# A planned decoder-layer kernel: intermediate values written over their inputs, and buffer rings of new sizes

## The chip, the cores and the metric

The kernel runs on one core of a Trainium2 chip. The time is the device time of one launch in microseconds. Three runs of the kernel before gave 1340.83, 1343.05 and 1343.17 us, a median of 1343.05. A profile was taken of one more execution, whose time was 1342.45 us.

The names of engines in the profile: PE is the matrix engine (PEld its weight loads), DVE the vector engine, ACT the engine for activations, POOL the general engine (GpSimd), SP the engine that issues the DMAs.

## The reference

32 sequences of 128 tokens with 128 features, in fp32, go through one decoder layer with a layernorm behind each residual:

```python
x = _layernorm(x + _L0_attn_ref(x, L0_attn_weight))             # 16 heads, q = k = v = x, projected 2048 -> 128
x = _layernorm(x + _L0_xattn_ref(x, ctx_1024, ...))             # 16 heads, window of 64, biases, projection
x = _layernorm(x + _L0_ffn_ref(x, wqkv, ..., w1, b1, w2, b2))   # a stack of two layers, see below
```

Each of the two layers in the third line is: shift half of the features by one token, qkv, l2norm of q and k with a scale and rotary factors, local attention with 8 heads of 64, `x = x + o @ wo`; then again shift, layernorm, `a, g = split(h @ w1 + b1)`, `x = x + (a * gelu(g)) @ w2 + b2`.

## The kernel before, in words

The 32 sequences are cut into nine groups, `SIZES` (L21): seven of 4, one of 3, one of 1. A group goes through four stages, which are Python generators: `self_attention` (L528), `cross_attention` (L612), and `layer` (L953) for l = 0 and l = 1. Within a stage the work is done per sequence ("batch" in the code): `self_half` twice (L545), `cross_batch` (L678), `local_batch` (L766). What is done for a whole group at once is the loads, the transposes of the group, the layernorms (`layernorm`, L372), the projections and the feed-forward (`feed_forward`, L899). `finish` (L972) adds the residual around the two layers, normalises and stores.

Nothing is issued in the order in which it is written. Every step is entered into a plan by `op` (L80) with an engine, an estimated duration, and the values that it reads and writes. L992 to L1000 sort the stages' pieces into a list of priorities: a piece of stage k and group g stands at `STARTS[g]/G + k*LAG*CLOSE[g]`, and the pieces of one stage are drawn apart by `SPREAD[k]`. Then `Plan.issue` (L128) simulates the engines with the estimated durations, and at each step issues the operation that can start first; on one engine it takes the oldest of those that can start within `near` ns (default 80) of the first, and it looks no further than `ahead` operations past the oldest that is not yet issued (`AHEAD`, 250). The result is a fixed order for each engine.

A value (`Val`, L56) lives in a slot of a ring (`Ring`, L45), from the first operation that writes or holds it to the last that uses it. There are three rings that matter: `m`, the 8 PSUM banks, of which two are kept back; `big`, 18 SBUF buffers of 1032 floats, 5 kept back; `mid`, 19 SBUF buffers of 520 floats, 6 kept back. Two smaller ones hold whole groups: `xb` (x1 and the outcome of layer 0) and `xc` (x2), 4 each. "Kept back" is this test (L171):

```python
if len(q.free) < len(vs) + (0 if q.queue[q.head] in vs else q.keep):
    ok = False
```

An operation that needs new slots may take the last ones only for the value that is next in the ring's line; any other must leave `keep` slots free. So values out of line get at most 6 of `m`, 13 of `big` and 13 of `mid`.

The places that the change touches: the sum of the heads into `acc` (L605 to L609); the bias `yc` added to x1 into a new value `x1c` (L648), and the projection's sum into another `acc` (L669); the outcome of the attention of a layer, `xa` (L961, written in L893 to L897); in the feed-forward `xb = x + b2` (L901), then the shifted copy `h` (L907; the copy of the unshifted half is L739 on POOL, the shifted half is a matmul, L743, evicted in L747), `hn`, the layernorm of `h` (L908), and the sum into `dst` (L948); in `finish` a sum `acc` and an outcome `o` (L973).

Lines that come up in the prediction: L416 is the row maximum of the scores on DVE, L462 the exponentials of cross and local attention, L477 the transposes of the exponentials, L484 their eviction, L492 the masked copy of the eight heads (`eight_heads`), L507 the scores of self and cross attention, L554 and L583 the value product and the output product of self attention, L772 the qkv product, L789 the power of the norms on POOL, L800 the rotary product on POOL, L847 and L876 the scores and outputs of local attention, L922 and L942 the two products of the feed-forward.

Of the kernel before, what the change touches and what calls it, by code (L numbers as in the profile page):

```python
# [12 lines left out]
ALU = mybir.AluOpType  # L13
# [12 lines left out]

AHEAD = 250
LAG = 1.3  # L30
CLOSE = (1, 1, 1, 1, 1, 1, 1, 0.9, 0.95)
SPREAD = (1.3, 0.9, 0.7, 1.1)
LH, LD = 8, 64
INNER = LH * LD
HID = 341
# [192 lines left out]
def decoder_kernel(ctx: ExitStack, tc: tile.TileContext, a: dict, out: bass.AP):  # L228
# [6 lines left out]
    def ring(name, n, keep, shape, dtype=F32, pool=const):  # L235
        return Ring([pool.tile(shape, dtype, name=f"{name}{i}") for i in range(n)], keep)

    mring = ring("m", 8, 2, [P, 512], pool=ps)
    big = ring("big", 18, 5, [P, 1032])
    mid = ring("mid", 19, 6, [P, 520])  # L240
    vbring = ring("vb", 2, 1, [P, 4, 288])
    x1ring = ring("xb", 4, 1, [P, G, D])
    x2ring = ring("xc", 4, 1, [P, G, D])
    small = ring("sm", 24, 4, [P, 32])
    padring = ring("pad", 4, 1, [P, 2, 64], BF16)

# [125 lines left out]
    def layernorm(src, dst, n):  # L372
        st = Val(small)

        def stats():
            for j in range(n):
                nc.vector.bn_stats(st.t[:, 6 * j : 6 * j + 6], group(src.t)[:, j, :])

        op("DVE", n * 290, stats, [src], [st])
        mv = Val(small)  # L380

        def aggr():
            for j in range(n):
# [12 lines left out]

        op("POOL", 1100 + 260 * n, rest, [], [mv])

        def apply():
            x, y = group(src.t), group(dst.t)  # L400
            for j in range(n):
                nc.scalar.activation(
                    y[:, j, :], x[:, j, :], AF.Identity,
                    scale=mv.t[:, 8 + j : 9 + j], bias=mv.t[:, 12 + j : 13 + j],
                )

        op("ACT", 425 * n, apply, [src, mv], [dst])

    def two_banks():
        return [Val(mring, lambda t: t.rearrange("p (h k) -> p h k", h=4)) for _ in range(2)]  # L410
# [117 lines left out]
    def self_attention(g):  # L528
        xT = load_group(a["xt"], g)
        if g == 0:  # L530
            load_self()
        x0 = load_group(a["xg"], g)
        if g == 1:
            load_cross()
        acc, n = Val(mid), SIZES[g]
        for j in range(n):
            yT = eight_heads(xT, j)
            for hh in range(2):
                self_half(j, hh, x0, xT, acc, yT)
            yield  # L540
        x1 = Val(x1ring, lambda t: t.rearrange("p g d -> p (g d)"))
        layernorm(acc, x1, n)
        x1s[g] = x1

    def self_half(j, hh, x0, xT, acc, yT):  # L545

        zs = Val(big, lambda t: t.rearrange("p (h d) -> p h d", h=HH))
        op("POOL", 130, lambda: nc.gpsimd.memset(zs.t[:, :, D : D + 1], 1.0), [], [(zs, 2)])
# [52 lines left out]
        for n, ns in ((4, 1270), (2, 730), (1, 450)):  # L601
            op("POOL", ns,
               lambda n=n: nc.gpsimd.tensor_tensor(z(0, n), z(0, n), z(n, n), ALU.add),  # L603
               [], [zs], port=n > 1)
        y = lambda: group(acc.t)[:, j, :]  # L605
        first = lambda: group(x0.t)[:, j, :] if hh == 0 else y()
        op("POOL", 450,
           lambda: nc.gpsimd.tensor_tensor(y(), first(), z(0, 1)[:, 0, :], ALU.add),
           [zs, x0], [(acc, j)])  # L609


    def cross_attention(g):  # L612
# [30 lines left out]

        vT = Val(mid)
        op("PE", n * 228, values, [cT, w_cross], [vp], hold=[vT])
        op("ACT", 140 + 113 * n,
           lambda: nc.scalar.copy(vT.t[:, every], vp.t[:, every]), [vp], [vT])
        x1c = Val(mid)  # L648
        op("POOL", 316 * n,
           lambda: nc.gpsimd.tensor_tensor(  # L650
               group(x1c.t)[:, 0:n], group(x1.t)[:, 0:n],
               yc.unsqueeze(1).to_broadcast([P, n, D]), ALU.add),
           [x1, w_cross], [x1c], port=True)
        on = Val(mid)
        for j in range(n):
            cross_batch(j, qT, kT, vT, on)
            yield
        onT = turned(on, n)
        yp = Val(mring)

        def project():
            for j in range(n):
                nc.tensor.matmul(
                    yp.t[:, 128 * j : 128 * j + 128], group(onT.t)[:, j, :], woT,
                    start=True, stop=True,
                )

        op("PE", n * 228, project, [onT, w_cross], [yp])
        acc = Val(mid)  # L669
        op("DVE", 160 + 135 * n,  # L670
           lambda: nc.vector.tensor_tensor(
               acc.t[:, every], yp.t[:, every], x1c.t[:, every], ALU.add),
           [yp, x1c], [acc])
        x2 = Val(x2ring, lambda t: t.rearrange("p g d -> p (g d)"))
        layernorm(acc, x2, n)
        x2s[g] = x2

    def cross_batch(j, qT, kT, vT, on):  # L678
# [87 lines left out]
    def local_batch(l, j, xin, hT, xout):  # L766
# [119 lines left out]
        def project():  # L886
            for i in range(4):
# [2 lines left out]
                    start=(i == 0), stop=(i == 3),  # L890
                )

        op("PE", 4 * 228, project, [onT, w_layer[l]], [yp], hold=[xout])  # L893
        op("DVE", 290,
           lambda: nc.vector.tensor_tensor(
               group(xout.t)[:, j, :], yp.t[:, 0:D], group(xin.t)[:, j, :], ALU.add),
           [yp, xin], [(xout, j)])  # L897

    def feed_forward(l, xg, dst, n):  # L899
        every = slice(0, 128 * n)  # L900
        xb = Val(mid)  # L901
        op("POOL", 316 * n,
           lambda: nc.gpsimd.tensor_tensor(
               group(xb.t)[:, 0:n], group(xg.t)[:, 0:n],
               b2[l].unsqueeze(1).to_broadcast([P, n, D]), ALU.add),
           [xg, w_layer[l]], [xb], port=True)
        h = shifted(xg, n)  # L907
        hn = Val(mid)  # L908
        layernorm(h, hn, n)
        tp, hT = Val(mring), Val(mid)  # L910
        op("PE", 113 * n, turn(hn, tp, n), [hn], [tp], hold=[hT])
        op("DVE", 160 + 135 * n,
           lambda: nc.vector.tensor_scalar(
               hT.t[:, every], tp.t[:, every], cols[:, 2 + 2 * l : 3 + 2 * l],
# [24 lines left out]
        def project():  # L939
# [4 lines left out]
                        w2[l][:m, c, :], start=(c == 0), stop=(c == 2),  # L944
                    )

        op("PE", 3 * 228 * n, project, us + [w_layer[l]], [yp], hold=[dst])
        op("DVE", 160 + 135 * n,  # L948
           lambda: nc.vector.tensor_tensor(dst.t[:, every], yp.t[:, every], xb.t[:, every], ALU.add),
           [yp, xb], [dst])  # L950


    def layer(l, g, xin):  # L953
        if g == 0:
            if l + 1 < DEPTH:
                load_layer(l + 1)
            prepare_layer(l)
        n = SIZES[g]
        hT = turned_shifted(xin, n)
        last = l == DEPTH - 1  # L960
        xa = Val(mid)  # L961
        xf = Val(mid) if last else Val(x1ring, lambda t: t.rearrange("p g d -> p (g d)"))
        for j in range(n):
            local_batch(l, j, xin, hT, xa)
            yield
        feed_forward(l, xa, xf, n)
        if last:
            finish(g, xf, n)
        else:
            xfs[g] = xf  # L970

    def finish(g, xf, n):  # L972
        acc, o, every = Val(mid), Val(mid), slice(0, 128 * n)  # L973
        op("POOL", 316 * n,
           lambda: nc.gpsimd.tensor_tensor(
               acc.t[:, every], xf.t[:, every], x2s[g].t[:, every], ALU.add),
           [xf, x2s[g]], [acc], port=True)
        layernorm(acc, o, n)
        op("SP", P * 512 * n / 380,
           lambda: nc.sync.dma_start(  # L980
               out_dram[:, STARTS[g] : STARTS[g] + n], group(o.t)[:, 0:n]), [o], [])

# [14 lines left out]
    for _, k, g, stage in sorted(todo, key=lambda t: t[:3]):  # L997
        if (k, g) not in running:
            running[k, g] = stage(g)
        next(running[k, g], None)  # L1000
    plan.issue(ahead=AHEAD)


def _constants():
# [96 lines left out]
```

## Time and profile before

| what | value |
|---|---|
| median of three runs | 1343.05 us |
| the profiled execution: its time | 1342.45 us |
| its span, from the first to the last instruction | 1340.7 us |
| mean granted clock of PE | 0.987 |
| instructions | 25686 |

The page of the profile gives the busy time of each engine as a share of the span: PE 94%, DVE 76%, ACT 74%, POOL 67%, PEld 63%. The DMA engines are busy in the first slice (0.6) and next to nothing afterwards. The answers of the trace that are quoted further on are of four kinds: busy time per stretch of the span ("windows"), groups of equal instructions with the number, the busy time and the mean duration, the waits of an engine, and the chain that ended last, in pieces: start, duration, what, and how many instructions. The PE's matmul records overlap where they are pipelined, and their ends are modelled; the pace of a stretch without gaps is its length divided by its number of matmuls.

### The profile page before, as it was taken

The page shows a single profiled execution, that of the slowest core. Times are in us where ns is not written, and L with a number is a line of the kernel's source. Part 1 is how long each engine was busy: PE and PEld are TensorE (multiplying, and loading weights), DVE is VectorE, ACT ScalarE, POOL GpSimd, SP SyncE. Part 2 cuts the span into 40 slices and gives each one's busy share as a digit, 9 for nine tenths or more (in the row PEclk, how much of TensorE's full clock was granted, in tenths as well). Part 3 has the DMA queues.
Part 4 walks back from the last instruction along what each step waited for, and adds up shares of the span by engine and source line. Part 5 has one row for each costly group of instructions (what it writes and reads, how often), then busy time and mean ns, then how long its engine had stood idle before and what let it go on. Part 6 is the DMA issues. An engine that isn't in the chain of part 4 may idle for free.

```text
span 1340.7 us, 25686 instructions
## 1 busy us (share of the span) xinstructions
PE 1265.2 (94%) x9314; PEld 847.3 (63%) x9314; DVE 1020.6 (76%) x1963; ACT 992.4 (74%) x2841; POOL 900.5 (67%) x1070
## 2 busy tenths in 40 slices
PE   8899999999999998999999999999999989999986
PEld 4656666766666665756666665666665576676655
DVE  2656788688877877877876887778877887888673
ACT  4355676777778777787787877867878698998874
POOL 3794875777686757867786667685766554868543
PEclk9999999999999999999999999999999999999988
DMA  6000000000000000000000000000000000000000
GB/s 229 1 1 1 17 9 1 2 17 4 7 1 9 9 1 16 1 1 17 1 17 1 13 1 19 1 3 1 7 9 1 3 1 9 1 2 1 9 1 17
DMA packets 9118, 15.59 MB, mean 12 GB/s; under 512 B 672, under 2 KB 5536, under 8 KB 8736
## 3 DMA queue, kind: packets, MB, share of 16 engines
q1 hardware_dynamic: 8992, 13.95, 3.2%
q8 instruction: 74, 1.21, 0.4%
q14 instruction: 52, 0.43, 0.1%
HBM read 11.85 MB, written 2.10 MB: 10 GB/s over the span
## 4 chain that ended last, share of the span: by engine, by line
PE 65%; ACT 12%; DVE 11%; POOL 9%; issue 2%; DMA 0%; POOLq 0%; DVEq 0%; SPq 0%; ACTq 0%
PE m L772 8%; PE m L583 7%; PE m L507 7%; PE m L554 6%; PE m L477 6%; ACT big L462 5%; PE m L847 4%; PE m L876 4%; PE m L922 4%; PE m L700 3%; PE m L942 3%; PE m L888 3%; PE m L827 3%; DVE big L862 2%; DVE sm L416 2%; POOL sm L789 2%
## 5 line engine op out<-in xcount | busy, mean ns | idle before, releaser
L462 ACT ACTIVATE big<-m,sm 128x128 f32<-128x128 f32 x1024 | 320.8, 405 | 52.6 <-DVE sm L416 47.4
L416 DVE TENSOR_REDUCE sm<-m 128x4 f32<-128x512 f32 x384 | 244.9, 682 | 110.8 <-PE m L507 40.2
L800 POOL TENSOR_TENSOR big<-big,layer_w 128x512 f32<-128x512 f32 x128 | 166.3, 1300 | 86.8 <-ACT big L777 74.6
L603 POOL TENSOR_TENSOR big<-big 128x512 f32<-128x512 f32 (+2 forms) x192 | 163.5, 852 | 83.2 <-DVE big L593 31.5
L789 POOL TENSOR_TENSOR sm<-sm,nhalf 128x16 f32<-128x16 f32 x64 | 198.4, 3100 | 25.2 <-DVE sm L786 21.0
L772 PE MATMUL m<-layer_w,mid 128*128 128x512 f32 x384 | 188.6, 602 | 4.5 <-ACT big L462 2.3
L477 PE MATMUL m<-ident,big 128*128 128x128 f32 x1024 | 147.3, 280 | 26.5 <-DVE big L862 13.3
L477 PEld LDWEIGHTS m<-ident,big 128*128 128x128 f32 x1024 | 116.9, 143 | 76.5 <-issue 33.6
L492 POOL TENSOR_TENSOR big<-mid,self_w 128x1024 f32<-128x1024 f32 x64 | 126.5, 1982 | 15.1 <-ACT mid L629 9.1
L507 PE MATMUL m<-big,mid 64*128 64x512 f32 x512 | 134.5, 614 | 0.0
L583 PEld LDWEIGHTS m<-big,big 128*128 128x128 f32 x1024 | 121.6, 193 | 17.1 <-issue 5.2
L583 PE MATMUL m<-big,big 128*128 128x129 f32 x1024 | 129.6, 280 | 2.3 <-DVE big L593 2.3
L554 PE MATMUL m<-self_w,mid 128*128 128x512 f32 x256 | 124.7, 604 | 6.5 <-DMA self_w<-in_self_w 5.9
L462 ACT ACTIVATION_READ_ACCUMULATOR big<-m,sm 128x1 f32 x512 | 120.2, 235 | 0.0
L862 DVE TENSOR_TENSOR big<-big,sm 128x512 f32<-128x512 f32 x128 | 108.8, 850 | 4.4
L593 DVE TENSOR_TENSOR big<-m,sm 128x384 f32<-128x384 f32 (+1 forms) x192 | 98.6, 514 | 6.8 <-DVE sm L592 0.3
L561 ACT COPY big<-m 128x512 f32<-128x512 f32 x128 | 74.8, 596 | 36.3 <-PE m L554 35.0
L484 DVE COPY big<-m 128x512 f32<-128x512 f32 x128 | 82.2, 682 | 23.6 <-PE m L477 23.2
L484 ACT COPY big<-m 128x512 f32<-128x512 f32 x128 | 76.0, 605 | 31.3 <-PE m L477 29.8
L809 DVE TENSOR_TENSOR big<-big,layer_w 128x1024 f32<-128x1024 f32 x64 | 83.3, 1302 | 20.3 <-ACT big L777 18.6
L833 ACT COPY big<-m 128x512 f32<-128x512 f32 x128 | 71.4, 604 | 31.2 <-PE m L827 30.9
L772 PEld LDWEIGHTS m<-layer_w,mid 128*128 128x128 f32 x384 | 64.1, 190 | 47.1 <-issue 32.5
(112 smaller groups left out, 2488.9 us busy)
## 6 DMA issues: line engine op xcount, KB each, us to landing
layer_w<-in_layer_w SPq DMA_DIRECT2D x2, 1877.0 KB, 11.8
mid<-in_xt SPq DMA_DIRECT2D x7, 256.0 KB, 3.1
mid<-in_xg SPq DMA_DIRECT2D x7, 256.0 KB, 3.0
mid<-in_ct SPq DMA_DIRECT2D x7, 256.0 KB, 3.2
out<-mid SPq DMA_DIRECT2D x7, 256.0 KB, 2.3
self_w<-in_self_w SPq DMA_DIRECT2D x1, 516.0 KB, 4.5
self_w<-in_self_w SPq DMA_DIRECT2D x1, 512.0 KB, 5.9
cross_w<-in_cross_w SPq DMA_DIRECT2D x1, 329.5 KB, 6.8
```

Source lines behind the costliest of these rows:

```text
L416: lambda b=b: nc.vector.tensor_reduce(nm.t[:, 4 * b : 4 * b + 4], s[b].t, AX.X, ALU.max, negate=True),
L462: nc.scalar.activation(e.t[:, h, :], s[b].t[:, h - 4 * b, :], AF.Exp, bias=nm.t[:, h : h + 1], accum_out=sums.t[:, h : h + 1] if sums else ...
L477: nc.tensor.transpose(tp.t[:, 128 * c : 128 * c + 128], e.t[:, 4 * b + c, :], ident)
L484: lambda: copy(et.t[:, 4 * b : 4 * b + 4, :], tp.t.rearrange("p (c k) -> p c k", c=4)),
L507: nc.tensor.matmul(s[b].t, group(stationary.t)[r, j, :], moving.t[r, 4 * hh : 4 * hh + 4, :], start=True, stop=True, tile_position=(64 * b ...
L554: lambda zp=zp, h0=h0: nc.tensor.matmul(zp.t, group(xT.t)[:, j, :], attn_w[:, h0 : h0 + 4, :], start=True, stop=True),
L583: nc.tensor.matmul(oz.t[:, i, :], e.t[:, h0 + i, :], zs.t[:, h0 + i, :], start=True, stop=True,)
L603: lambda n=n: nc.gpsimd.tensor_tensor(z(0, n), z(0, n), z(n, n), ALU.add),
L772: lambda hp=hp, i=i: nc.tensor.matmul(hp.t, group(hT.t)[:, j, :], wqkv[l][:, INNER * i : INNER * (i + 1)], start=True, stop=True),
L789: nc.gpsimd.tensor_tensor(rn.t[:, 0:16], rn.t[:, 0:16], nhalf, ALU.pow)
L800: nc.gpsimd.tensor_tensor(r2.t[:, :, :, d0 : d0 + 32], q[:, :, :, d1 : d1 + 32], tabs[l][:, :, d0 : d0 + 32].unsqueeze(2).to_broadcast([P, ...
L862: nc.vector.tensor_tensor(e.t[:, 4 * b : 4 * b + 4, :], e.t[:, 4 * b : 4 * b + 4, :], r.unsqueeze(2).to_broadcast([P, 4, P]), ALU.mult)
```

## The change

- Values are written over an input. Self attention sums into `x0`, the loaded group, in place of `acc`; cross attention adds `yc` to `x1` and the projection to the same `x1`, which stays until the layernorm into x2 has read it; layer 1 (the second) writes its attention outcome over its input; layer 0 keeps `xa` as a new value, but in the ring `xb` rather than `mid`. In the feed-forward the layernorm of `h` is written over `h`, `b2` is added to x in place, and the sum goes to the same value. In `finish` the sum, the layernorm and the store use the one value.
- In the feed-forward the order of two steps is exchanged: the shifted copy `h` is entered before the sum with `b2`, which now writes over what the copy reads.
- The rings: `big` 18 to 22, `mid` 19 to 16 with 5 kept back rather than 6, `xb` 4 to 8, `xc` 4 to 6. In bytes of a partition: 18*4128 + 19*2080 + 8*2048 = 130208 before, 22*4128 + 16*2080 + 14*2048 = 152768 after. `m` stays at 8 with 2 kept back.
- The planner's settings: `AHEAD` 250 to 230, `near` 80 to 60, the last of `CLOSE` 0.95 to 0.9 (the group of one), the last of `SPREAD` 1.1 to 1.5 (layer 1).

No instruction is added or taken away, and none gets another shape.

```diff
-AHEAD = 250
+AHEAD = 230
 LAG = 1.3
-CLOSE = (1, 1, 1, 1, 1, 1, 1, 0.9, 0.95)
-SPREAD = (1.3, 0.9, 0.7, 1.1)
+RINGS = (22, 16, 8, 6)
+KEEP = (2, 5, 5)
+NEAR = 60
+CLOSE = (1, 1, 1, 1, 1, 1, 1, 0.9, 0.9)
+SPREAD = (1.3, 0.9, 0.7, 1.5)
...
-    mring = ring("m", 8, 2, [P, 512], pool=ps)
-    big = ring("big", 18, 5, [P, 1032])
-    mid = ring("mid", 19, 6, [P, 520])
+    mring = ring("m", 8, KEEP[0], [P, 512], pool=ps)
+    big = ring("big", RINGS[0], KEEP[1], [P, 1032])
+    mid = ring("mid", RINGS[1], KEEP[2], [P, 520])
...
-    x1ring = ring("xb", 4, 1, [P, G, D])
-    x2ring = ring("xc", 4, 1, [P, G, D])
+    x1ring = ring("xb", RINGS[2], 1, [P, G, D])
+    x2ring = ring("xc", RINGS[3], 1, [P, G, D])
...
-        op("ACT", 425 * n, apply, [src, mv], [dst])
+        op("ACT", 425 * n, apply, [mv] + ([src] if src is not dst else []), [dst])
...
-        y = lambda: group(acc.t)[:, j, :]
-        first = lambda: group(x0.t)[:, j, :] if hh == 0 else y()
+        y = lambda: group(x0.t)[:, j, :]
         op("POOL", 450,
-           lambda: nc.gpsimd.tensor_tensor(y(), first(), z(0, 1)[:, 0, :], ALU.add),
-           [zs, x0], [(acc, j)])
+           lambda: nc.gpsimd.tensor_tensor(y(), y(), z(0, 1)[:, 0, :], ALU.add),
+           [zs], [(x0, j)])
...
-        x1c = Val(mid)
         op("POOL", 316 * n,
            lambda: nc.gpsimd.tensor_tensor(
-               group(x1c.t)[:, 0:n], group(x1.t)[:, 0:n],
+               group(x1.t)[:, 0:n], group(x1.t)[:, 0:n],
                yc.unsqueeze(1).to_broadcast([P, n, D]), ALU.add),
-           [x1, w_cross], [x1c], port=True)
+           [w_cross], [x1], port=True)
...
-        xb = Val(mid)
+        h = shifted(xg, n)
         op("POOL", 316 * n,
            lambda: nc.gpsimd.tensor_tensor(
-               group(xb.t)[:, 0:n], group(xg.t)[:, 0:n],
+               group(xg.t)[:, 0:n], group(xg.t)[:, 0:n],
                b2[l].unsqueeze(1).to_broadcast([P, n, D]), ALU.add),
-           [xg, w_layer[l]], [xb], port=True)
-        h = shifted(xg, n)
-        hn = Val(mid)
-        layernorm(h, hn, n)
+           [w_layer[l]], [xg], port=True)
+        layernorm(h, h, n)
...
-        xa = Val(mid)
-        xf = Val(mid) if last else Val(x1ring, lambda t: t.rearrange("p g d -> p (g d)"))
+        xa = xin if last else Val(x1ring, lambda t: t.rearrange("p g d -> p (g d)"))
...
-    plan.issue(ahead=AHEAD)
+    plan.issue(ahead=AHEAD, near=NEAR)
```

More of the change, by code (lines that the diff above doesn't have):

```diff
@@ L534, in self_attention @@
             load_cross()
-        acc, n = Val(mid), SIZES[g]
+        n = SIZES[g]
         for j in range(n):
@@ L538, in self_attention, with self_half @@
             for hh in range(2):
-                self_half(j, hh, x0, xT, acc, yT)
+                self_half(j, hh, x0, xT, yT)
             yield
         x1 = Val(x1ring, lambda t: t.rearrange("p g d -> p (g d)"))
-        layernorm(acc, x1, n)
+        layernorm(x0, x1, n)
         x1s[g] = x1
-    def self_half(j, hh, x0, xT, acc, yT):
+    def self_half(j, hh, x0, xT, yT):
         zs = Val(big, lambda t: t.rearrange("p (h d) -> p h d", h=HH))
@@ L668, in cross_attention @@
         op("PE", n * 228, project, [onT, w_cross], [yp])
-        acc = Val(mid)
         op("DVE", 160 + 135 * n,
            lambda: nc.vector.tensor_tensor(
-               acc.t[:, every], yp.t[:, every], x1c.t[:, every], ALU.add),
-           [yp, x1c], [acc])
+               x1.t[:, every], yp.t[:, every], x1.t[:, every], ALU.add),
+           [yp], [x1])
         x2 = Val(x2ring, lambda t: t.rearrange("p g d -> p (g d)"))
-        layernorm(acc, x2, n)
+        layernorm(x1, x2, n)
         x2s[g] = x2
@@ L891, in project @@
                 )
-        op("PE", 4 * 228, project, [onT, w_layer[l]], [yp], hold=[xout])
+        op("PE", 4 * 228, project, [onT, w_layer[l]], [yp], hold=[xout] if xout is not xin else [])
         op("DVE", 290,
@@ L896, in local_batch, with feed_forward @@
                group(xout.t)[:, j, :], yp.t[:, 0:D], group(xin.t)[:, j, :], ALU.add),
-           [yp, xin], [(xout, j)])
-    def feed_forward(l, xg, dst, n):
+           [yp] + ([xin] if xout is not xin else []), [(xout, j)])
+    def feed_forward(l, xg, n):
         every = slice(0, 128 * n)
-        xb = Val(mid)
+        h = shifted(xg, n)
         op("POOL", 316 * n,
            lambda: nc.gpsimd.tensor_tensor(
-               group(xb.t)[:, 0:n], group(xg.t)[:, 0:n],
+               group(xg.t)[:, 0:n], group(xg.t)[:, 0:n],
                b2[l].unsqueeze(1).to_broadcast([P, n, D]), ALU.add),
-           [xg, w_layer[l]], [xb], port=True)
-        h = shifted(xg, n)
-        hn = Val(mid)
-        layernorm(h, hn, n)
+           [w_layer[l]], [xg], port=True)
+        layernorm(h, h, n)
         tp, hT = Val(mring), Val(mid)
-        op("PE", 113 * n, turn(hn, tp, n), [hn], [tp], hold=[hT])
+        op("PE", 113 * n, turn(h, tp, n), [h], [tp], hold=[hT])
         op("DVE", 160 + 135 * n,
@@ L945, in project @@
                     )
-        op("PE", 3 * 228 * n, project, us + [w_layer[l]], [yp], hold=[dst])
+        op("PE", 3 * 228 * n, project, us + [w_layer[l]], [yp])
         op("DVE", 160 + 135 * n,
-           lambda: nc.vector.tensor_tensor(dst.t[:, every], yp.t[:, every], xb.t[:, every], ALU.add),
-           [yp, xb], [dst])
+           lambda: nc.vector.tensor_tensor(xg.t[:, every], yp.t[:, every], xg.t[:, every], ALU.add),
+           [yp], [xg])
     def layer(l, g, xin):
@@ L965, in layer @@
             yield
-        feed_forward(l, xa, xf, n)
+        feed_forward(l, xa, n)
         if last:
-            finish(g, xf, n)
+            finish(g, xa, n)
         else:
-            xfs[g] = xf
+            xfs[g] = xa
     def finish(g, xf, n):
-        acc, o, every = Val(mid), Val(mid), slice(0, 128 * n)
+        every = slice(0, 128 * n)
         op("POOL", 316 * n,
            lambda: nc.gpsimd.tensor_tensor(
-               acc.t[:, every], xf.t[:, every], x2s[g].t[:, every], ALU.add),
-           [xf, x2s[g]], [acc], port=True)
-        layernorm(acc, o, n)
+               xf.t[:, every], xf.t[:, every], x2s[g].t[:, every], ALU.add),
+           [x2s[g]], [xf], port=True)
+        layernorm(xf, xf, n)
         op("SP", P * 512 * n / 380,
            lambda: nc.sync.dma_start(
-               out_dram[:, STARTS[g] : STARTS[g] + n], group(o.t)[:, 0:n]), [o], [])
+               out_dram[:, STARTS[g] : STARTS[g] + n], group(xf.t)[:, 0:n]), [xf], [])
     x1s, x2s, xfs = {}, {}, {}
```

## The prediction

> **What bounds the kernel now.** I read the page first, its busy shares and its chain.
>
> ```profile
> span 1340.7 us, 25686 instructions
> PE 1265.2 (94%) x9314; PEld 847.3 (63%) x9314; DVE 1020.6 (76%) x1963; ACT 992.4 (74%) x2841; POOL 900.5 (67%) x1070
> PE 65%; ACT 12%; DVE 11%; POOL 9%; issue 2%; DMA 0%; POOLq 0%; DVEq 0%; SPq 0%; ACTq 0%
> ```
>
> PE is busy 94% of the span, so it idles 75.5 us in all. DMA has no share in the chain: loads don't matter. Next the windows, cut where stages begin and end (local attention begins at 164 us, self attention ends at 992, cross attention at 1150):
>
> ```profile
> 0.00:60.00 60.00, 50.60 (x254) 29.57 (x255) 24.80 (x57) 25.24 (x48) 31.09 (x70) 0.97 0.34 129
> 60.00:164.00 104.00, 101.24 (x757) 66.13 (x756) 70.43 (x181) 59.37 (x162) 76.31 (x128) 1.00 0.02 6
> 164.00:992.00 828.00, 798.63 (x6031) 534.72 (x6029) 659.32 (x1256) 627.88 (x1811) 587.47 (x666) 1.00 0.03 7
> 992.00:1150.00 158.00, 146.67 (x1114) 100.11 (x1115) 126.26 (x214) 129.86 (x396) 92.20 (x87) 0.98 0.01 3
> 1150.00:1341.00 191.00, 168.07 (x1166) 116.73 (x1165) 139.84 (x259) 150.06 (x428) 113.43 (x122) 0.95 0.02 5
> ```
>
> The first busy column is PE. With all four stages mixed (164 to 992) it idles 29.4 of 828 us, 3.5%; in the end of the run, where only cross attention and layers, then only layers are left, 34.3 of 349 us, 9.8%.
>
> **A rule that changes the size.** By the row, nothing that feeds PE better can give more than 75 us. The Trainium skill (Perfetto Trace Analysis, Identifying the Most-Contended Engine) says that a matmul engine's busy share is no measure of how near it is to its limit, since matmuls are pipelined. The chain has stretches in which PE never waited, and so its pace:
>
> ```profile
> 266.54 3.57 PE m L583 x32
> 270.12 0.87 PE m L477 x8
> 270.99 1.72 PE m L772 x4
> 272.71 0.44 PE m L368 x4
> 273.15 1.72 PE m L772 x4
> 274.87 5.15 PE m L922 x12
> 280.01 1.02 PE m L700 x16
> ```
>
> That is 0.112 us for one L583, 0.109 for L477, 0.43 for L772 and L922, 0.064 for L700. Counts times pace: L772 384 x 0.43 = 165; L554 256 x 0.43 = 110; L583 1024 x 0.112 = 115; L477 1024 x 0.109 = 112; L507 512 x 0.215 = 110; L700, L847 and L876 1024 x 0.066 each, 203; L922 83; L888 57, L827 56, L942 46; the small ones 130 together. Sum 1187 us. So 1341 - 1187 = 154 us are lost, twice what the page shows as idle: a gap shows only what is longer than a matmul's modelled tail. I keep both sizes.
>
> **Is it buffers that PE lacks?** The same page (Optimization Strategy) says that repeated gaps on the engine that should be full can mean too little SBUF or PSUM for the next tile. By that rule, taken to its end, all 75 or 154 us are within this change's reach. I counted it. The n-th instruction of a line belongs to the n-th value in the program's order, so the trace gives each value's first and last use. From 164 to 992 us, 12.8 values of the 19 of `mid` live at a time; the limit for values out of line is 13, and it is reached 65% of the time. `big` holds 10.5 of 18, at its limit of 13 for 19% of the time. From 1150 us on, `mid` holds 8.2 and `big` 5.4: there SBUF is no limit. Then each gap of PE over 60 ns, 114 of them, 61.5 us: in 34.6 us some matmul had its inputs and lacked only a PSUM slot; in 5.2 us both a PSUM and a `mid` slot; in 12.2 us nothing was ready, in 9.5 us something was ready and stood behind another. No gap of PE was for `big`. So the rule holds for PSUM, which the change leaves as it is, and for SBUF with 5.2 of 61.5 us, 8.5%.
>
> **The change part by part.**
>
> *Values in place, instructions the same.* No count and no shape changes. L608, L650, L671, L903, L949 and L975 keep their operands' memories. In-place forms are in the trace already: on POOL L603 takes 1.33 us for 512 columns, L800, which writes elsewhere, 1.30; on DVE L813 takes 1.31 us for 1024, L809 1.30. So the bounds are -2% and +2% of the groups that change (34 + 11 + 18 + 9 us on POOL), +-1.5 us, beside PE; I take 0.
>
> *New waits.* L650 now overwrites x1, so it waits for the transposes of x1 (L368, 0.44 us for four). Behind it on POOL stand L681 and L492 of the next batch, and PE's L507 waits for those. The chain holds 0 us of L650 and of L671. In the feed-forward, the sum with b2 (L903) waits for the shift matmul L743 (0.40 us), and behind it stands whatever POOL has next; DVE's L949 needs it only after twelve L922 (5.15 us) and L942 (2.88 us), which cover it. Without this cover it would cost 18 x 0.4 = 7 us at most. 0 taken.
>
> *Copy before sum.* L903 (1.09 us median) no longer stands ahead of the copy L739 (0.4 us) to which the layernorm waits. At most 18 x 1.09 = 19.6 us of latency, but the chain's pieces hold 1.05 us of L903 in all: PE had other groups' matmuls meanwhile. I take -1.
>
> *Room.* The values taken out of `mid` held, from their lives in the trace: acc 0.62, x1c 0.83, xa 0.87, xb 0.34, hn, the last xf and finish's two 0.13 together, cross acc 0.05 of a slot each on the mean, 2.8 in all. The limit out of line falls from 13 to 11. So the mean falls from 12.8 to about 10 against 11: one slot of air in place of 0.2. In `big` the limit rises from 13 to 17 with nothing moved. `xb` and `xc` never held over 3 and 4 values; in `xb` x1 now stays some 100 us longer (x1c's life was 124 us) and xa from the start of layer 0 to the store, about 2 more on the mean, of 8: no limit. Worth: between 0 (the air is filled with work that runs ahead, as self attention's zs, which live 64 us each) and what SBUF blocked. By the idle row that is 5.2 us; by the pace, if the unseen half is lost in the same proportion, 8.5% of 154 = 13 us. I take 9, the middle, because `mid` is at its limit where PE is densest and losses there are short ones. POOL was short of `big` or `mid` in 27 us of its 412 us idle; at POOL's 9% of the chain, -2.5.
>
> *Settings.* `near` 60 follows the earliest start more closely, AHEAD 230 looks less far, which counts where the rings don't limit first. SPREAD and CLOSE move layer 1 of groups 6 and 7 apart and the last group of one forward by 0.2 group periods. The trace of before can't show another order. From both sides: if the 9.8% of idle of the last 349 us became the middle's 3.5%, -22; if layer work slid into the end, + (rival 3). I take 0.
>
> Sum: -1 - 9 - 2.5 = -12.5 us on 1342.45, which is 1330; the profiled execution lies 0.6 below the median, so 1330.5 against the runs. I say 1331.
>
> **The rivals.**
>
> 1. *As summed*: 1331, 1319 to 1340. Chance 0.50.
> 2. *The new order also mends the end.* For it: PE's waits there are short and in one place (L477 for DVE's L862, 10.5 of its 13.3 us, after 992), more sequences side by side would fill them, and no ring forbids. Against: ACT is busy 150 of 191 us in the last window, so there is not much to add. 1331 - 22 = 1309. Chance 0.20.
> 3. *The run ahead is longer and the end gets heavier.* `big` lets self attention run further ahead (up to 4 more zs), and SPREAD 1.5 puts layer 1's sequences later, so more are left when nothing else can be mixed in. Price: a sequence's layer is 10 us of PE at pace (L772, L827, L841, L847, half of L477, L876, L888, L922 and L942: 625 us for 64, 9.8 each, and the group's transposes). The same sum of counts times pace, taken window by window, is 757 us of work in 828 us (0.915) in the middle and 151 in 191 (0.79) at the end. 10/0.79 - 10/0.915 = 1.7 us for each sequence that slides. It eats the 12.5 us from 7 sequences on and at 12 gives 1331 + 20 = 1351. For it: ACT and PE are nearly equally loaded in the end. Against: AHEAD is smaller. Chance 0.20.
> 4. *PSUM is the only limit that counts*, 35 of 61.5 us, and it keeps all of it: 1343. Chance 0.10.
>
> A difference within 0.2% (2.7 us) is about what a measurement of this kernel can't tell from none. Faster by more 0.70, within 0.10, slower by more 0.20. The range, 1305 to 1352, leaves out the far ends of 2 and 3.
>
> **What would show it.** Right: 25686 instructions give or take table loads, POOL's and DVE's busy time unchanged within 1%, PE's idle time about 10 us less, and the gain between 164 and 992 us, with self attention ending earlier by about that; the 349 us behind it unchanged. Rival 2: PE over 93% busy after the end of self attention. Rival 3: self attention ends clearly before 980, and yet the last stretch is longer than 349 us by more than was won. Rival 4: the middle as long as before with fuller `big`. Wrong altogether: more table loads on ACT (32 now at 1.28 us each), or slower in-place forms.

## The result, and the profile after

Over 20 runs of each on one chip the kernel after took 1341.24 us (median; 1334.42 to 1343.96), the kernel before 1343.11 (1340.83 to 1348.33): a ratio of 0.9979, 95% interval 0.9967 to 0.9992. The change gives 2 us, 0.2%. The forecast was 1331, so it is 10 us too low.

The page of the kernel after, its span, busy shares and chain:

```profile
span 1340.8 us, 25604 instructions
PE 1268.5 (95%) x9291; PEld 850.5 (63%) x9314; DVE 1023.2 (76%) x1963; ACT 982.7 (73%) x2831; POOL 890.4 (66%) x1070
PE 67%; DVE 14%; ACT 8%; POOL 7%; issue 2%; DMA 0%; DVEq 0%; SPq 0%; POOLq 0%; ACTq 0%
```

Weight loads, DVE and POOL instructions are as many as before. The 23 missing matmuls are missing records, as the weight loads show; ACT has ten fewer, which are table loads. DVE is busy 0.3% more and POOL 1.1% less, where the prediction had both within 1%. PE is busy 3 us more, so its visible idle time fell from 75.5 to 72.3 us, by 3 us where 10 were expected. The same windows as in the prediction (the first busy column is PE):

```profile
0.00:60.00 60.00, 50.71 (x264) 29.27 (x265) 27.34 (x67) 24.27 (x47) 34.51 (x75) 1.00 0.34 128
60.00:164.00 104.00, 101.03 (x757) 66.42 (x757) 69.72 (x175) 63.66 (x172) 74.31 (x122) 1.00 0.02 6
164.00:992.00 828.00, 801.28 (x6034) 536.16 (x6048) 659.17 (x1242) 618.78 (x1796) 577.66 (x668) 1.00 0.02 7
992.00:1150.00 158.00, 152.46 (x1120) 103.58 (x1126) 131.65 (x245) 135.10 (x406) 98.26 (x97) 0.99 0.01 3
1150.00:1341.00 191.00, 163.00 (x1122) 115.12 (x1124) 135.37 (x239) 140.85 (x411) 105.61 (x112) 0.91 0.02 6
```

Up to 1150 us PE is ahead by 8.3 us of busy time (2.65 in the middle, 5.8 in the next stretch); in the last 191 us it is behind by 5.1, and the granted clock (the first number behind the POOL column) is 0.91 where it was 0.95. Cut where the stages of this kernel end, self attention at 973 us and cross attention at 1123:

```profile
160.00:973.00 813.00, 786.35 (x5879) 523.57 (x5891) 644.98 (x1225) 605.33 (x1753) 567.03 (x658) 1.00 0.02 7
973.00:1123.00 150.00, 144.57 (x1157) 102.88 (x1161) 128.20 (x225) 128.74 (x403) 95.68 (x90) 0.99 0.01 4
1123.00:1341.00 218.00, 189.82 (x1257) 130.93 (x1260) 156.23 (x281) 164.18 (x467) 122.75 (x131) 0.92 0.02 6
```

Self attention ends 19 us earlier than before and cross attention 27 us earlier. That is mostly work put off, not time won. In the 813 us PE gets through 7.25 weight loads per us (5891 in all), in the 828 us of before through 7.28 (6029). By 992 us it has done 7070 loads, before 7040: 30 more, some 4 us at that pace. Behind the end of self attention stand 2421 loads in place of 2280; the 141 more are some 19 us of work. The stretch with layers alone has become 218 us in place of 191, with 95 more weight loads in it, and PE idles 28 us there in place of 23.

The room in SBUF came as forecast. Counted as in the prediction, `mid` holds 9.9 values between 164 and 992 us (12.8 before, 10 forecast) and reaches its former limit of 13 for 3% of the time (65% before). The gaps of PE in which a matmul lacked an SBUF slot went from 5.2 us to 0. Those in which it lacked only a PSUM slot hardly changed: 34.6 and 37.7 in the count of the prediction, 35.0 and 33.3 when each gap is judged at its middle.

### The profile page after: what moved, and what is told of

It is laid out like the page before. It is cut to its first block, busy times and chain, and to the rows that moved or that the text cites. A ratio compares the mean times of both kernels' runs of the same rounds, so it can differ in the third digit from the quotient of the medians.

```text
span 1340.8 us, 25604 instructions
## 1 busy us (share of the span) xinstructions
PE 1268.5 (95%) x9291; PEld 850.5 (63%) x9314; DVE 1023.2 (76%) x1963; ACT 982.7 (73%) x2831; POOL 890.4 (66%) x1070
## 4 chain that ended last, share of the span: by engine, by line
PE 67%; DVE 14%; ACT 8%; POOL 7%; issue 2%; DMA 0%; DVEq 0%; SPq 0%; POOLq 0%; ACTq 0%
PE m L772 8%; PE m L557 7%; PE m L480 7%; PE m L510 7%; PE m L586 6%; PE m L920 6%; ACT big L465 5%; PE m L847 4%; PE m L876 4%; PE m L700 4%; PE m L888 3%; DVE sm L419 3%; PE m L940 3%; POOL sm L789 3%; PE m L827 3%
## 5 line engine op out<-in xcount | busy, mean ns | idle before, releaser
L465 ACT ACTIVATE big<-m,sm 128x128 f32<-128x128 f32 x1024 | 321.5, 403 | 74.3 <-DVE sm L419 64.2
L862 DVE TENSOR_TENSOR big<-big,sm 128x512 f32<-128x512 f32 x128 | 100.9, 788 | 4.4
L816 DVE TENSOR_TENSOR big<-big,sm 128x1024 f32<-128x1024 f32 x64 | 95.7, 1495 | 4.2 <-POOL sm L790 1.8
```

The costliest lines, as they stand in the source:

```text
L465: nc.scalar.activation(e.t[:, h, :], s[b].t[:, h - 4 * b, :], AF.Exp, bias=nm.t[:, h : h + 1], accum_out=sums.t[:, h : h + 1] if sums else ...
```

## The theories and the experiments

Theory A: the order of issue decides by tens of microseconds, both kernels stand at settings that suit their own rings, and room is worth some 10 us at like settings. Theory B: PSUM alone limits, room is worth nothing. Theory C: room pays, and the new SPREAD eats it at the end. D, E and F came later and are stated where they are used. Every ratio is to the kernel before, run beside it on the same chip. "Fitted" are settings at which the planner's own schedule came out short, "unfitted" all others.

| run | what | us, median | ratio, 95% interval |
|---|---|---|---|
| e1 | before, new settings | 1370.32 | 1.0201 (1.0178 to 1.0223) |
| e2 | after, old settings | 1365.10 | 1.0165 (1.0150 to 1.0180) |
| e3 | after, old rings | 1390.48 | 1.0336 (1.0302 to 1.0369) |
| e4 | before, big 22 | 1373.18 | 1.0229 (1.0211 to 1.0246) |
| e5 | before, AHEAD 248 | 1384.44 | 1.0308 (1.0288 to 1.0328) |
| e6 | before, AHEAD 252 | 1394.48 | 1.0388 (1.0367 to 1.0408) |
| e7 | after, AHEAD 228 | 1363.71 | 1.0154 (1.0137 to 1.0171) |
| e8 | after, AHEAD 232 | 1352.48 | 1.0072 (1.0056 to 1.0089) |
| e9, e10 | halfway settings, AHEAD 240: before, after | 1392.69, 1404.75 | 1.0375 (1.0359 to 1.0390), 1.0464 (1.0448 to 1.0479) |
| e11, e12 | the same, AHEAD 242: before, after | 1376.66, 1366.53 | 1.0256 (1.0239 to 1.0273), 1.0180 (1.0165 to 1.0195) |
| e17, e18 | the same, AHEAD 238: before, after | 1385.50, 1395.82 | 1.0325 (1.0303 to 1.0346), 1.0396 (1.0380 to 1.0412) |
| e13 | before, order held, more slots | 1338.94 | 0.9975 (0.9964 to 0.9985) |
| e14 | after, other settings 1 | 1344.79 | 1.0007 (0.9997 to 1.0018) |
| e15 | after, other settings 2 | 1335.02 | 0.9938 (0.9917 to 0.9959) |
| e16 | after, AHEAD 231, near 65 | 1339.48 | 0.9980 (0.9966 to 0.9994) |

### The parts of the change, one without the other

```diff
 # e1, in the kernel before
-AHEAD = 250
+AHEAD = 230
-CLOSE = (1, 1, 1, 1, 1, 1, 1, 0.9, 0.95)
-SPREAD = (1.3, 0.9, 0.7, 1.1)
+CLOSE = (1, 1, 1, 1, 1, 1, 1, 0.9, 0.9)
+SPREAD = (1.3, 0.9, 0.7, 1.5)
-    plan.issue(ahead=AHEAD)
+    plan.issue(ahead=AHEAD, near=60)
 # e2, in the kernel after: the same four back
 # e3, in the kernel after
-RINGS = (22, 16, 8, 6)
-KEEP = (2, 5, 5)
+RINGS = (18, 19, 4, 4)
+KEEP = (2, 5, 6)
 # e4, in the kernel before
-    big = ring("big", 18, 5, [P, 1032])
+    big = ring("big", 22, 5, [P, 1032])
```

> The kernel before with the four new settings alone (AHEAD 230, near 60, CLOSE and SPREAD of the change); values and rings as before. Theory A (the room is worth some 10 us at like settings, and each kernel stands at settings that suit its own rings): 1355 to 1375, since these settings were not fitted to these rings. Theory B (PSUM is the only limit, the room is worth nothing): as after, 1341, within 5. Theory C (SPREAD 1.5 makes the end heavier and eats what the room gives): a little slower than before, 1348 to 1353, with the loss all after the end of self attention.

> The kernel after (values in place, new rings) with the four settings of before. Theory A: slower than after, 1350 to 1370, since any other settings than the fitted ones cost, but faster than the run with the new settings in the kernel before. Theory B: 1343, within 5. Theory C: faster than after, 1328 to 1334, because the end is as light as before and the room still pays.

> The kernel after with rings of before (big 18, mid 19 with 6 kept back, xb 4, xc 4), in place and with the new settings. xb at 4 is tight for values that stay there longer. Theory A: slower than after by 10 to 40, 1351 to 1381. Theory B: 1341, within 5, as SBUF doesn't bind. Theory C: 1341 to 1350.

> The kernel before with big at 22 in place of 18 and nothing else. No gap of PE was for big in the trace of before. Theory A: the order changes all over, so the time moves by more than 5 us, more likely up (1350 to 1365), although there is only more room. Theory B and C: 1343, within 3.

e1 to e3 each have a part of the change without the rest, and cost 22 to 48 us; all of it together gains 2. Theory A's numbers hold in e1, e2 and 10 us beyond in e3. B is out: with the new rings and values in place, settings alone move the time by 24 us (e2 against after). C is out: SPREAD and the others set back made it slower, not faster. e4 is the barest of them: four more buffers, nothing taken away, and 30 us more, 8 beyond what A had expected. e3 against e1 is the values in place alone, 20 us slower, but with `xb` at 4, which is tight for them; no run has the values without the rings at settings of their own.

### The nearest settings

```diff
-AHEAD = 250
+AHEAD = 248     # e5; 252 in e6; in the kernel after 228 in e7, 232 in e8
```

> The kernel before with AHEAD 248 in place of 250, nothing else. Theory A (each kernel stands on a fitted setting, and any other order costs): 1355 to 1375. Theory B (PSUM alone limits, two operations of lookahead out of 250 mean nothing): 1343, within 3.

> The kernel before with AHEAD 252. Theory A: 1355 to 1380; that more lookahead is worse too would say that 250 isn't on a slope but a lucky point. Theory B: 1343, within 3.

> The kernel after with AHEAD 228 in place of 230. Theory A: 1350 to 1367; and if the room pays at like settings, the mean of this and the next lies some 10 us below the mean of the two runs of the kernel before with AHEAD 248 and 252. Theory B: 1341, within 3.

> The kernel after with AHEAD 232. Theory A: 1345 to 1365. Theory B: 1341, within 3.

Two operations of lookahead more or fewer, of 250, cost the kernel before 41 and 52 us, more than A had said in both; the kernel after loses 22 and 11, as A had said. Their mean lies 31 us below that of e5 and e6, where A had said some 10. So AHEAD 250 lies on no slope: it is a low point with higher ones on both sides. Where e6 loses its 50 us shows in the windows (those of before are in the prediction):

```profile
60.00:164.00 104.00, 97.83 (x728) 64.00 (x725) 68.20 (x173) 55.04 (x151) 72.97 (x124) 0.98 0.02 6
164.00:992.00 828.00, 788.33 (x5895) 525.43 (x5893) 651.03 (x1235) 613.43 (x1768) 564.09 (x655) 1.00 0.02 7
```

In the same 828 us PE gets through 5893 weight loads where it was 6029, and idles 40 us in place of 29: a little of it in many places. With rings as before and `mid` at its limit for as much of the time (60%, 65% before), it has 0.7 us of gaps for want of SBUF (5.2 before), but 54.1 us for want of a PSUM slot alone (34.6 before).

### Pairs at settings fitted to neither

AHEAD 240, near 70, the last of CLOSE 0.925 and of SPREAD 1.3, halfway between the two kernels; then AHEAD 242 and 238. Theory D: room gives nothing by itself, and what differs is only which order was hit.

> The kernel before with settings halfway between its own and the new ones (AHEAD 240, near 70, the last of CLOSE 0.925, the last of SPREAD 1.3), fitted to neither kernel. Theory A, which holds that each kernel was fitted by its settings and that the room pays at like settings: 1375 to 1400, as its other unfitted settings gave (1370 to 1394). Theory B (PSUM alone, room worth nothing): the same as the kernel after at these settings, within 5. Theory D (new: the room pays nothing by itself, and what differs is only which order was hit): anything in 1350 to 1400, with the kernel after above it as often as below.

> The kernel after with the same halfway settings. Theory A: below the kernel before at the same settings by 5 to 30, so 1350 to 1385. Theory B: the same within 5. Theory D: above or below with equal chance.

> The kernel before at the halfway settings with AHEAD 242. Theory A: 1365 to 1395. Theory D: more than 5 us from the run with 240, in any direction.

> The kernel after at the halfway settings with AHEAD 242. Theory A: below the kernel before at 242, 1350 to 1375. Theory D: above or below with equal chance. If the mean of the two differences, after less before at 240 and 242, is between -20 and 0, theory A's size of about 10 us stays possible; two pairs can't show more.

> The kernel before at the halfway settings with AHEAD 238 (near 70, the last of CLOSE 0.925, of SPREAD 1.3). The third pair at settings fitted to neither. Unfitted settings gave 1370 to 1394 in this kernel: 1370 to 1395.

> The kernel after at the same settings. If the room and the values in place are worth some 10 us on the mean (theory A), below the run before by 0 to 25 more likely than not; if they are worth nothing beyond the 3 us that a held order shows (theory D), above as often as below. With differences of +12 and -10 from the first two pairs, a third between -15 and +15 leaves the mean open.

A's ranges held in e9, e11, e12 and e17. They failed in e10, which is 20 us above its range, and in e18, which A had below its pair. D, with the kernel after above as often as below, is not contradicted. After less before: +12.1, -10.1, +10.3 us, a mean of +4 with a standard error of 7. Taking all unfitted settings together (e1, e5, e6, e9, e11, e17 for the kernel before: mean 1384.0, scatter 9.5; e2, e7, e8, e10, e12, e18 for the one after: 1374.7, scatter 20.8), the difference is -9 +- 9 (standard error). Such intervals (95%: some +-30 with three pairs, +-20 with six against six) rule out neither the 12.5 us of the forecast nor nothing. What the new values and rings are worth on the mean stays open in the runs.

The slowest, e10, differs from the fast ones in what PE waits for. The waits of PE in e10, longest in total first (total us, times, longest):

```profile
PE m L480 <- DVE big L862: 18.8, 20, 3.0
PE m L440 <- POOL pad L434: 11.8, 9, 4.7
```

These two were 13.3 and 5.1 us before (L477 for L862, L437 for L431): the transposes of the exponentials wait for their division on DVE, and self attention's maxima for POOL. While PE waits for the maxima, the scores of self attention hold their PSUM banks, and in 74.3 us of e10's gaps something was ready that lacked only such a bank. Over all 20 kernels this count and the span go together (correlation 0.90: 34.6 us at 1341, 46.3 at 1362, 54.1 at 1391, 74.3 at 1404), and the count of gaps for want of SBUF, made in the same way, does not (0.25, never over 9 us). But all gaps together go with the span more closely still (0.97), so the count doesn't single PSUM out; and it is a count, not a trial. All 8 banks are in the ring already, and neither fewer banks nor another number kept back was tried.

### The order held, the buffers spread

```diff
-    def __init__(self, tiles, keep):
+    def __init__(self, tiles, keep, spare=0):
         self.tiles, self.keep = tiles, keep
-        self.free = [(0.0, i) for i in range(len(tiles))]
+        self.free = [(0.0, i) for i in range(len(tiles) - spare)]
+        self.slots = [(0.0, i) for i in range(len(tiles))]
...
-                    v.slot = f[1]
+                    v.turn = f[1]
+                    at = min(v.ring.slots)
+                    v.ring.slots.remove(at)
+                    v.slot = at[1]
...
-                    v.ring.free.append((v.end, v.slot))
+                    v.ring.free.append((v.end, v.turn))
+                    v.ring.slots.append((v.end, v.slot))
...
-    big = ring("big", 18, 5, [P, 1032])
-    mid = ring("mid", 19, 6, [P, 520])
+    big = ring("big", 22, 5, [P, 1032], spare=4)
+    mid = ring("mid", 22, 6, [P, 520], spare=3)
```

The planner counts 18 and 19 as before, so the order is the same on every engine; only the place where a value lies is taken from more.

> The kernel before with its order of issue kept as it is on every engine, and only the buffers behind it spread over more slots: big 22, mid 22, while the planner still counts 18 and 19. Theory E (room acts only through the order that it allows; no instruction of a given order waits for a slot that counts): 1342.5, within 2. Theory F (waits for a freed buffer sit in the order as it stands): 1330 to 1337, as the forecast had it for the room.

It gains 3.4 us (0.15% to 0.36%), between the two theories, and neither explains it. As the order is the same, the two profiled executions can be laid over each other operation by operation. The lead comes in steps: 1.1 us between 202 and 206 us, 1.5 at 395, some 0.3 us each at 505, 534 and 538. The first two, 2.6 of 3.8 us, are no waits for a slot. The timeline of the kernel before at the first step (start, duration, engine and line):

```profile
200.58 0.17 DVE L861 RECIPROCAL sm<-sm 128x4 f32<-128x4 f32 x1
200.81 2.81 POOL L603 TENSOR_TENSOR big<-big 128x512 f32<-128x512 f32 x3 [3.84 <-DVE sm L861]
200.85 1.78 DVE L862 TENSOR_TENSOR big<-big,sm 128x512 f32<-128x512 f32 x1
202.78 1.07 PE L477 MATMUL m<-ident,big 128*128 128x128 f32 x8 [0.70 <-DVE big L862]
```

and of e13 (lines moved by 5):

```profile
200.53 0.17 DVE L866 RECIPROCAL sm<-sm 128x4 f32<-128x4 f32 x1
200.72 0.69 DVE L867 TENSOR_TENSOR big<-big,sm 128x512 f32<-128x512 f32 x1
200.76 3.54 POOL L608 TENSOR_TENSOR big<-big 128x512 f32<-128x512 f32 x3 [3.84 <-DVE sm L866]
201.95 1.09 PE L482 MATMUL m<-ident,big 128*128 128x128 f32 x8
```

DVE's division has both inputs in SBUF, and POOL's three additions read SBUF. Where POOL starts 0.04 us ahead, DVE takes 1.78 us for what otherwise takes 0.69, and PE waits 0.70 us; where DVE starts 0.04 us ahead, the additions take 3.54 for 2.81 (the first of them 1.79 for 1.27), and PE does not wait. At 393 us it is the same again: POOL's L492 at 393.00 and DVE's L862 at 393.04 in the kernel before, 2.39 us for the latter. L603 and L862 write in place and take no slot; L492 takes one, but starts as soon as POOL is free in both executions. So 2.6 of the 3.8 us between these two executions are two meetings of DVE and POOL that fell out the other way. The steps at 534 and 538, 0.6 us, lie where the granted clock is 0.50: for 6.8 us in the kernel before (531.3 to 538.1), for 3.4 us in e13. What slots gave by themselves is at most the remaining 0.6 us. Why the new places shifted those starts by some hundredths of a microsecond no run shows.

### Other settings for the new rings

```diff
 # e14
+AHEAD = 242, NEAR = 65, CLOSE = (1, 1, 1, 1, 1, 1, 1, 1.0, 1.05), SPREAD = (1.4, 1.0, 0.5, 1.3)
 # e15
+AHEAD = 250, NEAR = 60, LAG = 1.35, CLOSE = (1, 1, 1, 1, 1, 1, 1, 0.85, 0.8)
+SPREAD = (1.1, 1.0, 1.0, 1.4), RINGS = (21, 18, 8, 5)
 # e16
+AHEAD = 231, NEAR = 65
```

These were taken because the planner's own schedule came out shortest for them among many settings.

> The kernel after with other fitted settings: AHEAD 242, near 65, CLOSE ending 1.0 and 1.05, SPREAD 1.4, 1.0, 0.5, 1.3; rings as after. If the order is what decides, and such settings can be found by fitting: 1330 to 1350. If only a neighbourhood of the settings of after is good: 1355 to 1380.

> The kernel after with a second set of fitted settings: AHEAD 250, LAG 1.35, CLOSE ending 0.85 and 0.8, SPREAD 1.1, 1.0, 1.0, 1.4, rings 21, 18, 8, 5. Expected as for the first set: 1330 to 1350, or 1355 to 1380 if only one neighbourhood is good.

> The kernel after with AHEAD 231 and near 65. AHEAD 228 and 232 cost 22 and 11 us. If settings act by chance and not by their size, this point between can be as good as after: 1335 to 1348.

All three came out as fitted settings should, 1335 to 1345, where none of the twelve unfitted ones came below 1352. e16 lies between 228 and 232, which cost 22 and 11 us.

The planner's totals are no times, but they tell much of what the runs show. The latest `end` in `Plan.issue`, worked out from the text of each kernel, is 1316.3 us for the kernel before and 1314.5 for the one after; 1349.0, 1342.5, 1354.2 and 1347.9 for e1 to e4; 1334 to 1370 for the twelve unfitted kernels and 1312 to 1313 for e14 to e16. Over the 19 different orders it goes with the measured time (correlation 0.97, scatter about a line 5.6 us). So which order is good is not a lottery that only the chip can decide. The planner's difference of before and after, 1.8 us, agrees with the measured 1.9 better than that scatter warrants. At 80 settings drawn at random, the same for both kernels, its totals are 8.4 us lower on the mean for the kernel after (standard error 1.6, scatter from pair to pair 14). That would be theory A's size; it is planned time, an estimate, and no run shows it.

e15 beats both kernels: 0.9938 of before (0.9917 to 0.9959, which doesn't reach the interval of the kernel after). Its windows, cut at the ends of its own stages (956 and 1092 us):

```profile
176.00:956.00 780.00, 750.97 (x5599) 502.72 (x5607) 611.89 (x1171) 583.80 (x1676) 544.24 (x634) 0.99 0.02 7
956.00:1092.00 136.00, 130.81 (x1071) 91.37 (x1073) 121.39 (x205) 117.23 (x367) 91.13 (x83) 1.00 0.01 4
1092.00:1334.00 242.00, 215.56 (x1519) 148.87 (x1527) 183.71 (x333) 193.57 (x565) 148.38 (x149) 0.98 0.02 5
```

Its layer-only end is the longest of the three kernels, 242 us, and yet PE is busy 89% there (87% after, 88% before) at a clock of 0.98. So a long end need not cost; how much PE waits in it matters too.

## Why the prediction was wrong

**What bounds the kernel** was read rightly in the main: PE with many short waits, and PSUM rather than SBUF behind most visible gaps. Of the 154 us that the pace shows as lost, up to 18 are clock, for which the prediction had no term: the granted clock of the profile before is at half for 36.5 us (see below). Rival 4 (1343, chance 0.10) came nearest to the outcome by luck. It has a new order worth nothing, and e1 to e8 show an order to be worth tens of us.

**The step that failed is "Settings", taken at 0 and added to "Room".** With +20 and -22 as its ends, the term treated the order of before as one like any other, and the sum took each term as worth the same alone and beside the other. Four kernels show that it isn't. The new settings cost 28 us in the old rings (e1 against before) and save 24 in the new (after against e2), both beyond those ends. The new values and rings cost 22 us at the old settings (e2 against before) and save 29 at the new (after against e1). The kernel before stood at a low point: its six other settings gave 1370 to 1394, 27 to 52 us above its own. A change that makes the planner choose once anew, even four more buffers (e4), leaves that point, and the new settings are a low point of the new rings. So the term was the largest of the sum, with either sign, and what was measured is the distance between two low points, 2 us. The prediction says rightly that the trace of before can't show another order. The planner's totals above could have shown it before any run.

**"Room", -9 and -2.5, was too large.** The buffers came as forecast (`mid` 12.8 to 9.9, SBUF-starved gaps 5.2 us to 0); the microseconds did not. By 992 us, where the gain was to be, PE is some 4 us ahead. The 5.2 us were gaps in which PSUM was short too, as the prediction has it, and PSUM stayed short (34.6 to 37.7 us). With the order held, more slots give 3.4 us in all, of which at most 0.6 are theirs in the profiled pair (e13). The scaling from 5.2 to 13 us by the unseen half has no support in the runs. What room is worth on the mean over orders stays open (-9 +- 9 or +4 +- 7 in the runs, -8 in the planner's totals).

**The end.** The prediction expected 349 us behind the end of self attention, unchanged. It is 368 (1341 less 973), longer by the 19 us by which self attention ends earlier, as work was moved there. That is half of rival 3's sign: self attention ends before 980, but the rest is longer by just as much, not by more. Rival 3's price of 1.7 us for each sequence that slides was not tried. Part of the loss there is clock. The windows of the kernel after:

```profile
1150.00:1190.00 40.00, 34.88 (x234) 24.08 (x234) 35.11 (x41) 31.91 (x86) 32.31 (x25) 0.87 0.02 7
1270.00:1310.00 40.00, 31.37 (x229) 23.48 (x230) 27.54 (x51) 31.64 (x112) 18.81 (x18) 0.84 0.00 1
```

and of the kernel before:

```profile
1150.00:1190.00 40.00, 38.33 (x264) 26.09 (x263) 36.14 (x59) 36.34 (x100) 28.84 (x28) 1.00 0.01 2
1270.00:1310.00 40.00, 34.68 (x250) 24.55 (x246) 28.29 (x46) 28.46 (x83) 15.64 (x14) 0.91 0.00 1
```

The granted clock is lower in windows in which PE is busy less. These values are means of two steps. Cut at the steps themselves, with the time before beside it, the kernel after has:

```profile
1166.00:1176.00 10.00, 8.75 (x49) 5.07 (x48) 9.69 (x9) 9.16 (x16) 9.75 (x6) 1.00 0.00 1
1177.41:1187.64 10.23, 7.38 (x45) 5.59 (x46) 10.10 (x15) 6.70 (x33) 4.59 (x4) 0.50 0.00 0
```

The same sixteen matmuls in the first of these windows and in the second:

```profile
1172.91 1.16 PE L847 MATMUL m<-big 64*128 64x128 f32 x16
1183.22 2.08 PE L847 MATMUL m<-big 64*128 64x128 f32 x16
```

In the traces of all 20 kernels the clock is either 1.0 or 0.5. The kernel after has it at 0.5 for 46.0 us, 39.1 of them behind the end of self attention; the kernel before for 36.5 and 26.3 us. The 12.8 us more in the end are at most 6.4 us of matmul time, an estimate from the halved pace. Waits come first: in these two kernels each such stretch begins after 3.4 us in which PE idled 1.6 us or more, in waits none of which was longer than 3.3 us (the last stretch of each follows the last matmul). PE's waits from 1150 us on, of the kernel after:

```profile
PE m L480 <- DVE sm L861: 5.9, 3, 3.2
PE m L480 <- ACT big L465: 2.9, 3, 2.3
```

Before, the longest single wait there was 2.0 us. Over the 20 runs of the kernel after, the time falls by 7.7 us for each 0.01 of mean clock (correlation -0.95; 1334.4 us at 0.991, 1344.0 at 0.980). On that line it would stand at 1338 at the 0.987 of the profile of before. So 3 to 6 of the missing 10 us went with the clock. As a low clock itself follows waits, this is no cause apart from them.

**New waits and the exchange in the feed-forward, 0 and -1.** The bias of cross attention (L651) waited 2.0 us in two waits for the transposes of x1, and nobody waited for it. POOL does wait for the shift matmul, as said: L903 in the kernel after,

```profile
L903 POOL TENSOR_TENSOR xb<-xb,layer_w x18: 409/1092/1941, 262.6 to 1327.1; 128x512 f32<-128x512 f32 x14, 128x384 f32<-128x384 f32 x2, 128x128 f32<-128x128 f32 x2
...
  PE m L743: 12.3, 10
```

12.3 us in ten waits, where 7 was the bound; the bound had the matmul's duration and not the time for which the matmul itself stands in PE's order. The trace names nobody who waited for L903, so the wait cost nothing that shows, as taken. No run has the exchange alone; its -1 is untested. In-place forms: median 1.092 us against 1.089 for L903, 1.268 for both forms of the sum in `finish`, 0.457 against 0.454 for the sum of the heads. (Single long ones, up to 1.9 and 2.2 us, lift the means of the first two.) At the median the forms cost nothing, as taken.

**Table loads**, named as a thing that could spoil it, went the other way. The groups of the kernel after:

```profile
L926 ACT ACT_TABLE_LOAD x11 | 14.1, 1283 | 0.2
L465 ACT ACT_TABLE_LOAD x7 | 9.0, 1283 | 0.1
L578 ACT ACT_TABLE_LOAD x3 | 3.8, 1283 | 0.1
L564 ACT ACT_TABLE_LOAD x1 | 1.3, 1283 | 0.7 <-PEq L1088 0.7
```

22 in place of 32, 13 us of ACT less. What that is worth in time no run separates: ACT's share of the chain fell from 12% to 8%, DVE's rose from 11% to 14%.

## What to carry to other kernels

Where a planner writes the order, its settings are part of the kernel. A change of buffers must be weighed at several settings of both kernels, and terms read from the trace of one order can't be added up for another. The scatter between unfitted settings (10 to 20 us here) is then the floor of a forecast from that trace, with a sign against the change if the kernel before stands at a low point. The planner's own total costs no run and should be asked first; here it left a scatter of 5.6 us. Gaps for want of one resource are worth their length only if no other resource is short in the same moments. A stage that ends earlier is a gain only if the work done by then is more: count the loads.

## What was not expected of the hardware

- A DVE product with two SBUF inputs and a POOL addition on SBUF that start 0.04 us apart cost 1.1 us more on DVE or 0.5 us more on POOL, according to which is first (1.78 for 0.69, 1.79 for 1.27 us). The Trainium skill (SBUF — State Buffer, Who interferes with whom) has an exclusive lock here, for which a DVE instruction with two SBUF inputs and a GpSimd instruction that reads SBUF contend. The traces agree: the later one loses most of the other's length (1.1 of 1.27, 0.5 of 0.69 us). What they add is that it makes an unchanged order worth 1 to 1.5 us more or less at a single place.
- The granted clock falls to half for stretches of 3.4 us and more after single waits of 3.3 us and less, with 1.6 us or more of idle time in the 3.4 us ahead of it. The mean clock of one kernel ranged from 0.980 to 0.991 over 20 runs, and 9.5 us of time went with it, five times what the change gave.
